# A graph network's edge kernel: the sums of two pairs of edge blocks moved between the first layers of the two pairs

## The chip, the core and the metric

The kernel runs on one core of one Trainium2 chip. A core has five engines with a queue of instructions each: PE (the matrix engine, with its weight loads shown apart as PEld), DVE (vector), ACT (scalar), POOL (here it issues the indirect gathers) and SP (here it issues plain DMAs). An engine works through its queue in order and waits for another one by a semaphore. The metric is the device time of one launch in microseconds (us). A profiled execution gives the time of every instruction; its rows are quoted below.

## The reference

A network of 6,250 nodes with 256 values each and 206,250 edges. What is computed, cut to what matters:

```python
h = relu(layernorm(x))
e = relu(raw @ W_e1.T + b_e1) @ W_e2.T + b_e2          # raw: 64 values of an edge
edge_emb = (e * (polarity + 0.01)) @ W_le.T + b_le
msg = relu(h[src] + edge_emb)                          # one row of h per edge: a gather
aggr = segment_sum(msg, dst, num_segments=6250)        # edges come sorted by dst
x + W_g2 @ relu(layernorm((h + aggr) @ W_g1.T + b_g1)) # per node
```

All numbers are 32-bit floats. The second layer of an edge and `W_le` are one product in the kernel, since nothing nonlinear stands between them.

## The kernel before, in words

The edges are cut into blocks of 512; there are 403 blocks. Two blocks are a pair (`q`, 202 pairs, one DMA for the 64 raw values of both), and half a block (256 edges) is a unit (`u`), so a pair has four units. Almost the whole time goes to one loop over the units in `gnn_kernel`. No planner reorders anything: what the program calls first stands first in each engine's queue.

- **First layer**, `first_layer(q)` (lines 278 to 311): for each half `c` of the 256 outputs one matmul per block (L292, 64 rows by 128 columns of the array, 512 edges wide), so four instructions and four PSUM banks a pair. A 32-bit matmul instruction shows as two records in the profile, so a pair has 8 records and each of them a weight load. ACT reads three of the four banks (L308), DVE the fourth (L305), both into the tile `e`.
- **Second layer of a unit**, `edge_part(u)` (L317 to L334): four matmuls over the full array (L325, 8 records) into one PSUM bank, which DVE adds to `msg` (L331).
- **PSUM**: seven banks `pz` are handed out in a ring (`Ring`); who takes a bank waits until the reader of seven banks ago is done. The eighth bank, `pd`, holds the sums.
- **Message**, `whole(u)`: DVE multiplies by the polarity and adds the gathered rows (L685, tile `hg`), ACT takes the relu (L690).
- **Sums**, `sums` = `add_pairs` (L735 to L753) with `add_up`: per block four matmuls of 128 rows by 32 columns (L703), four of them side by side in the array, 256 wide, into `pd`. Two pairs make 16 instructions, 32 records. The first of a pair waits for the newest message of the pair (`newest`). After every third pair `keep` copies `pd` out on ACT (L718).
- **A turn**, `turn_of(q)`: after the second unit of each pair. In the first and last pairs (`by_two` false) it serves one pair; in the middle, on every second pair, it serves two: 95 such turns, each followed by eight units.
- **Gathers**: `in_step(us, behind)` (L646 to L652), called as `paced` by the first layer and by each unit. It adds the PE work just written down (`spent`: 1.754 us a unit, 0.9 a half of a first layer, 0.46 a block of sums, this one without a call of its own, 0.81 a step of node work) and issues as many gathers (L634, 128 rows of 1 KB each, on POOL) as this work allows at 1.288 us each, with 6 us of float. The first gather of such a call waits until the matmul `behind` is done, the rest follow in POOL's queue.
- **Node work**: transposes and small matmuls (L166, L181, L199, L212) for each group of 128 nodes, spread over the units by `at`, `soon` and `due`.

Of the kernel before, what the change touches and what calls it, by code (L numbers as in the profile page):

```python
# [100 lines left out]
def gnn_kernel(ctx: ExitStack, tc: tile.TileContext, x, src_c, dst_c, dst_r, pol_c, raw_t, w_e1t, w_e2,  # L101
# [37 lines left out]
    def behind(ins, other):  # L139

        if other is not None:
            tc.add_manual_dep(ins.ins, other.ins.name, mybir.DependencyInfo(
                mybir.DependencyClass.Sync, mybir.DependencyReason.DATA), reason="one wait for several")
# [93 lines left out]
    with fast:  # L237
# [35 lines left out]
        def load_pair(q):  # L273
            if q < NP:
                raw[q] = ld.tile([P, 512], F32, name="raw")
                nc.sync.dma_start(out=raw[q], in_=raw_t[q])

        def first_layer(q):

            bs = [b for b in (2 * q, 2 * q + 1) if b < NB]  # L280
            if not bs:
                return
            for b in bs:
                e1[b] = e1_p.tile([P, 2, 512], F32, name="e1")
            pe, z = {}, {}
            for c in range(2):
                olds = []
                for s, b in enumerate(bs):
                    pe[s, c] = ps().rearrange("p a b -> p (a b)")
                    olds.append(ps.old())  # L290
                for s, b in enumerate(bs):
                    z[c] = nc.tensor.matmul(pe[s, c], we1_s[s * F:(s + 1) * F, c * P:(c + 1) * P],  # L292
                                            raw[q][s * F:(s + 1) * F, :], start=True, stop=True)
                    ps.wrote(z[c], len(bs) - 1 - s)
                    reader, writer = olds[s]
                    if reader is not None and writer is not None:
                        tc.declare_no_dep(z[c].ins, writer.ins, reason="the bank's reader has waited for it")
                    if s == 0:
                        for reader, _ in olds[1:]:
                            behind(z[c], reader)  # L300
                paced(LAYER, z[c])
            for c in range(2):
                for s, b in enumerate(bs):
                    if s == c == 1:
                        a = nc.vector.tensor_scalar(e1[b][:, c, :], pe[s, c], be1_s[:, c:c + 1], 0.0, op0=ALU.add,  # L305
                                                    op1=ALU.max)
                    else:
                        a = nc.scalar.activation(e1[b][:, c, :], pe[s, c], AF.Relu, bias=be1_s[:, c:c + 1])  # L308
                    behind(a, z[c])
                    ps.read(a, len(bs) * (1 - c) + len(bs) - 1 - s)  # L310
            raw.pop(q)
# [28 lines left out]
        def by_two(q):  # L340
            return FEW <= q < NP - FEW

        def turn_of(q):


            if not by_two(q):
                if q + 2 < NP:
                    first_layer(q + 2)
                sums(q == NP - 1)
                load_pair(q + 4)  # L350
            elif q % 2 == 0:
                sums(False)
                first_layer(q + 2)
                first_layer(q + 3)
                load_pair(q + 4)
                load_pair(q + 5)

        def forward(u):

            edge_part(u)  # L360
            if u % 4 == TURN:
                turn_of(u // 4)
# [803 lines left out]
```

## Time and profile before

| | |
|---|---|
| median of three runs | 2580.09 us (2572.7 to 2583.99) |
| the profiled execution | 2579.07 us, span 2577.4 us |
| PE busy | 2314.6 us, 90% of the span |
| DVE busy | 1613.4 us, 63% |
| POOL busy | 1618.9 us, 63% |
| ACT busy | 1019.3 us, 40% |
| mean granted clock of PE | 0.946 |

In a row of groups stand the line, the engine, the operation, the tiles written and read, the shape and the count; behind the bar the busy time, the mean of one in ns, and the idle time of the engine just before them with what ended most of it. In a timeline row stand the start and length in us, then engine, line, operation, tiles, shape, the number of records merged into the row, and in brackets the idle time before it and what ended that. A row of waits gives the total in us, the number and the longest. The start of a PE record is when it was taken up; its end is modelled.

### The profile page before, as it was taken

How to read it: one execution, taken by the hardware profiler on the slowest of the kernel's cores; microseconds unless marked ns; L12 is line 12 of the kernel's file. 1: busy time of each engine (PE TensorE's matmuls, PEld its weight loads, DVE VectorE, ACT ScalarE, POOL GpSimd, SP SyncE). 2: the span in 40 equal slices, each digit the busy share in tenths (PEclk: the TensorE clock that was granted, in tenths of full speed). 3: DMA queues.
4: the chain of work that ended last, by engine and by line, in shares of the span. 5: the costliest groups of instructions: out<-in, count | busy, mean ns of one | idle time of the engine just before them, and what ended most of it. 6: DMA issues, size and time to landing. Idle time of an engine off the chain costs nothing.

```text
span 2577.4 us, 36784 instructions
## 1 busy us (share of the span) xinstructions
PE 2314.6 (90%) x11940; PEld 1634.7 (63%) x11940; DVE 1613.4 (63%) x3705; ACT 1019.3 (40%) x1804; POOL 1618.9 (63%) x1675
## 2 busy tenths in 40 slices
PE   9988999989989998988888999998989899888968
PEld 6666666666657666666666666665667566666646
DVE  7866666666656665665656565665656566656636
ACT  7443434343334434343433333343434334333423
POOL 6666666666656666666666666666666666666661
PEclk9899999999989999999999999999999999999989
DMA  9443444434444434443444444444434445443441
GB/s 306 139 135 113 121 123 131 130 115 133 125 118 136 132 112 129 129 132 112 125 125 122 132 134 118 122 130 129 136 115 117 129 123 148 117 132 114 121 119 47
DMA packets 176430, 330.30 MB, mean 128 GB/s; under 512 B 39055, under 2 KB 98280, under 8 KB 176232
## 3 DMA queue, kind: packets, MB, share of 16 engines
q0 software_dynamic: 77376, 211.39, 29.2%
q1 hardware_dynamic: 97556, 113.22, 13.7%
q10 hardware_dynamic: 1300, 3.28, 0.4%
q8 instruction: 95, 1.56, 0.2%
q14 instruction: 103, 0.84, 0.1%
HBM read 293.92 MB, written 33.82 MB: 127 GB/s over the span
## 4 chain that ended last, share of the span: by engine, by line
PE 81%; issue 8%; DVE 5%; another core or an unknown queue 3%; ACT 3%; DMA 0%; ACTq 0%; DVEq 0%
PE pz L325 50%; PE pz L292 17%; PE pd L703 8%; DVE hg L685 2%; PE pz L181 2%; PE pz L212 2%; DVE msg L331 1%; ACT e L308 1%; ACT hg L690 1%; PE pz L166 0%; PE pz L199 0%; DVE st L151 0%; DVE sel L663 0%; ACT xt L440 0%
## 5 line engine op out<-in xcount | busy, mean ns | idle before, releaser
L634 POOL DMA_INDIRECT hg<-hb_d,src_s x1604 | 1574.1, 981 | 897.5 <-issue 520.0
L325 PE MATMUL pz<-wc_s,e 128*128 128x256 f32 x6448 | 1494.5, 388 | 15.5 <-issue 13.0
L325 PEld LDWEIGHTS pz<-wc_s,e 128*128 128x128 f32 x6448 | 1236.4, 194 | 281.6 <-ACT e L308 65.1
L690 ACT ACTIVATE hg<-hg 128x512 f32<-128x512 f32 x805 | 507.5, 630 | 988.5 <-DVE hg L685 800.8
L331 DVE TENSOR_TENSOR msg<-pz,bc_s 128x512 f32<-128x512 f32 x799 | 545.0, 684 | 404.9 <-remote 163.5
L685 DVE SCALAR_TENSOR_TENSOR hg<-msg,pol_s,hg 128x256 f32<-128x256 f32 x1612 | 694.7, 476 | 0.4
L292 PE MATMUL pz<-raw,we_s 64*128 64x512 f32 x1612 | 487.4, 696 | 141.6 <-ACT e L308 86.8
L305 DVE TENSOR_SCALAR e<-pz,vecs 128x512 f32<-128x512 f32 x201 | 150.8, 750 | 504.6 <-PE pz L292 358.4
L308 ACT ACTIVATE e<-pz,vecs 128x512 f32<-128x512 f32 x605 | 367.0, 692 | 202.3 <-PE pz L292 147.9
L292 PEld LDWEIGHTS pz<-raw,we_s 64*128 64x128 f32 x1612 | 177.0, 210 | 395.6 <-issue 232.8
L703 PE MATMUL pd<-hg,sel 128*32 128x256 f32 x3216 | 259.2, 388 | 88.1 <-issue 81.1
L703 PEld LDWEIGHTS pd<-hg,sel 128*32 128x32 f32 x3216 | 110.9, 109 | 216.6 <-issue 163.4
L718 ACT ACTIVATE ms<-pd 128x256 f32<-128x256 f32 x66 | 25.3, 383 | 318.8 <-remote 133.2
L663 DVE SCALAR_TENSOR_TENSOR sel<-iota_w,zero_c,rel 128x128 f32<-128x128 f32 x403 | 137.8, 342 | 0.0
L181 PE MATMUL pz<-wg_s,hT 128*128 128x256 f32 (+1 forms) x196 | 52.8, 393 | 2.6 <-ACT hg L690 2.1
L212 PE MATMUL pz<-wg_s,nT 128*128 128x256 f32 (+1 forms) x196 | 50.8, 382 | 2.0 <-ACT nT L203 1.8
L181 PEld LDWEIGHTS pz<-wg_s,hT 128*128 128x128 f32 (+1 forms) x196 | 37.7, 195 | 10.4 <-ACT hg L690 2.5
L212 PEld LDWEIGHTS pz<-wg_s,nT 128*128 128x128 f32 (+1 forms) x196 | 36.8, 190 | 8.7 <-ACT nT L203 2.7
L444 POOL TENSOR_TENSOR hb<-xt,rows_b 128x256 f32<-128x256 f32 (+1 forms) x49 | 34.1, 728 | 10.5 <-ACT xt L440 4.4
L203 ACT ACTIVATE nT<-pz,vecs 128x128 f32<-128x128 f32 (+1 forms) x98 | 38.7, 444 | 2.6 <-PE pz L199 2.4
L800 DVE TENSOR_TENSOR stb<-stb,ab 128x256 f32<-128x256 f32 x94 | 38.7, 411 | 0.0
L230 DVE SCALAR_TENSOR_TENSOR xt<-xt,zero_c,rows_b 128x128 f32<-128x128 f32 (+1 forms) x98 | 33.5, 343 | 0.0
(108 smaller groups left out, 376.2 us busy)
## 6 DMA issues: line engine op xcount, KB each, us to landing
raw<-in_raw_t_dram SPq DMA_DIRECT2D x202, 256.0 KB
hg<-hb_d,src_s POOLq DMA_INDIRECT x1604
sum_d<-zrow SPq DMA_DIRECT2D x94, 128.0 KB
ab<-sum_d SPq DMA_DIRECT2D x94, 128.0 KB
sum_d<-ms SPq DMA_DIRECT2D x264, 32.0 KB
hb_d<-hb SPq DMA_DIRECT2D x12, 512.0 KB
xt<-in_x_dram SPq DMA_DIRECT2D x48, 128.0 KB
out_dram<-ot SPq DMA_DIRECT2D x48, 128.0 KB
```

The source lines that it names most:

```text
L181: z = nc.tensor.matmul(ph[:n, 0, :], aT[:, c, :n], wg1_s[:, c, :], start=c == 0 and not bias_by_pe, stop=c == 1)
L212: z = nc.tensor.matmul(po[:n, 0, :], nT[:, c, :n], wg2_s[:, c, :], start=c == 0, stop=c == 1)
L292: z[c] = nc.tensor.matmul(pe[s, c], we1_s[s * F:(s + 1) * F, c * P:(c + 1) * P], raw[q][s * F:(s + 1) * F, :], start=True, stop=True)
L305: a = nc.vector.tensor_scalar(e1[b][:, c, :], pe[s, c], be1_s[:, c:c + 1], 0.0, op0=ALU.add, op1=ALU.max)
L308: a = nc.scalar.activation(e1[b][:, c, :], pe[s, c], AF.Relu, bias=be1_s[:, c:c + 1])
L325: last_z = nc.tensor.matmul(pz[:, i, :], e1[b][:, c, k:k + P], wc_s[:, c, :], start=c == 0, stop=c == 1)
L331: ps.read(nc.vector.tensor_add(msg[u], pz, bc_s))
L634: g = nc.gpsimd.indirect_dma_start(out=hg[u][:, i, :], out_offset=None, in_=hb_d, in_offset=bass.IndirectOffsetOnAxis(ap=src_s[:, 2 * u + ...
L663: nc.vector.scalar_tensor_tensor(sel[g][:, k * S:(k + 1) * S, :], iota_w.rearrange("p (o w) -> p o w", o=1).to_broadcast([P, S, W]), zero_ ...
L685: product = nc.vector.scalar_tensor_tensor(hg[u][:, i, :], m[:, i, :], pol_s[:, 2 * u + i:2 * u + i + 1], hg[u][:, i, :], op0=ALU.mult, op ...
L690: done[u] = product, nc.scalar.activation(hg[u], hg[u], AF.Relu)
L703: z = nc.tensor.matmul(acc[g][j * W:(j + 1) * W, :], sel[g][:, k * S + j, :], m[:, j % 2, :], start=k == 0, stop=b == blocks_of(g)[-1])
```

## The change

In a turn for two pairs the call of the sums moves behind the first layer of the first of the two pairs. Nothing else is changed: every instruction is there as before, with the same operands but for the numbers of some buffers.

```diff
             elif q % 2 == 0:
+                first_layer(q + 2)
                 sums(False)
-                first_layer(q + 2)
                 first_layer(q + 3)
                 load_pair(q + 4)
                 load_pair(q + 5)
```

On PE a turn was: 32 records of sums, 16 records of first layer. It becomes: 8 records of first layer, 32 of sums, 8 of first layer. On ACT the copy of `pd` (L718), where a turn has one, moves from ahead of six reads of the first layer to between the third and the fourth. On DVE the order is the same. On POOL the order of the gathers is the same, but the matmuls that they wait for are others: `spent` has the four blocks' 1.84 us of sums added only ahead of the third of the four calls from the first layers, where before it was ahead of the first.

## The prediction

> **What bounds the kernel now.** I read the groups of instructions first (POOL's row from the page, PE's with their shapes apart), then the waits, then the timeline of single turns, PE and POOL apart.
>
> ```profile
> L634 POOL DMA_INDIRECT hg<-hb_d,src_s x1604 | 1574.1, 981 | 897.5 <-issue 520.0
> ...
> L325 PE MATMUL pz<-wc_s,e 128*128 128x256 f32 x6448 | 1494.5, 388 | 15.5 <-issue 13.0 <-ACT msg L329 1.1 <-DVE xt L230 0.9
> L292 PE MATMUL pz<-raw,we_s 64*128 64x512 f32 x1612 | 487.4, 696 | 141.6 <-ACT e L308 86.8 <-issue 44.8 <-DVE msg L331 6.7
> L703 PE MATMUL pd<-hg,sel 128*32 128x256 f32 x3216 | 259.2, 388 | 88.1 <-issue 81.1 <-ACT hg L690 5.2
> ```
>
> PE is the bound, and its second layer (L325) hardly ever waits: 15.5 us of 1494.5. The idle time stands before the first layer (L292) and the sums (L703), both of them in the turns. A turn that nothing disturbs shows what they cost by themselves (PE's rows, then POOL's):
>
> ```profile
> 1044.72 1.93 PE L703 MATMUL pd<-hg,sel 128*32 128x256 f32 x32
> 1046.58 3.70 PE L292 MATMUL pz<-raw,we_s 64*128 64x512 f32 x16
> 1050.22 1.99 PE L325 MATMUL pz<-wc_s,e 128*128 128x256 f32 x8
> ...
> 1042.53 0.95 POOL L634 DMA_INDIRECT hg<-hb_d,src_s  x1 [0.30 <-issue]
> 1045.23 0.95 POOL L634 DMA_INDIRECT hg<-hb_d,src_s  x1 [1.76 <-PE pz L325]
> ```
>
> It takes 1050.22 - 1044.72 = 5.50 us. Over the run L703 and L292 take 259.2 + 88.1 + 487.4 + 141.6 = 976.3 us, busy and idle. At the pace of the free turn they would take 3216/32 x 1.93 + 1612/16 x 3.70 = 567 us. So about 409 us, a sixth of the span, are lost in the turns, some 4.1 us in each; the modelled ends hide part of it as busy time. The usual turn looks like this (PE, ACT, POOL):
>
> ```profile
> 1240.14 1.93 PE L703 MATMUL pd<-hg,sel 128*32 128x256 f32 x32
> 1242.03 2.59 PE L292 MATMUL pz<-raw,we_s 64*128 64x512 f32 x8
> 1244.90 1.15 PE L292 MATMUL pz<-raw,we_s 64*128 64x512 f32 x4 [0.28 <-issue]
> 1247.35 1.13 PE L292 MATMUL pz<-raw,we_s 64*128 64x512 f32 x4 [1.30 <-ACT e L308]
> 1248.41 1.78 PE L325 MATMUL pz<-wc_s,e 128*128 128x256 f32 x7
> ...
> 1246.61 3.58 ACT L308 ACTIVATE e<-pz,vecs 128x512 f32<-128x512 f32 x6 [5.38 <-PE pz L292]
> ...
> 1243.82 0.95 POOL L634 DMA_INDIRECT hg<-hb_d,src_s  x1 [0.30 <-issue]
> 1247.25 0.94 POOL L634 DMA_INDIRECT hg<-hb_d,src_s  x1 [2.49 <-issue]
> ```
>
> The first matmuls of the first layer are through by about 1243, yet ACT, idle for 5.38 us, gets to read them only at 1246.61. What PE has done is told late. The last four records need a bank that ACT has to read first (seven banks, eight are needed), so PE stands from 1246.05 to 1247.35. The telling comes 1246.61 - 1243.82 = 2.79 us after POOL began its last free gather; POOL then stood because its next one hangs on the first layer. In the free turn POOL stood from 1043.48 to 1045.23, just when the sums began, and nothing was late. I read this as: sums issued while POOL gathers without a pause hold back what PE has to tell, until POOL runs out of gathers that it may start. Why that is so the trace does not say. In other turns PE itself gets stuck in the sums (PE, then POOL, then DVE):
>
> ```profile
> 1342.36 1.91 PE L703 MATMUL pd<-hg,sel 128*32 128x256 f32 x26
> 1345.24 0.38 PE L703 MATMUL pd<-hg,sel 128*32 128x256 f32 x1 [0.97 <-issue]
> ...
> 1348.09 0.63 PE L703 MATMUL pd<-hg,sel 128*32 128x256 f32 x3 [0.34 <-issue]
> 1348.65 3.70 PE L292 MATMUL pz<-raw,we_s 64*128 64x512 f32 x16
> 1352.29 1.99 PE L325 MATMUL pz<-wc_s,e 128*128 128x256 f32 x8
> ...
> 1345.22 0.94 POOL L634 DMA_INDIRECT hg<-hb_d,src_s  x1 [0.30 <-issue]
> 1350.08 0.94 POOL L634 DMA_INDIRECT hg<-hb_d,src_s  x1 [3.92 <-ACT ms L718]
> ...
> 1348.12 0.69 DVE L331 TENSOR_TENSOR msg<-pz,bc_s 128x512 f32<-128x512 f32 x1 [6.34 <-remote]
> ```
>
> Again it lets go 2.87 us after the start of POOL's last free gather (1348.09 - 1345.22), and 9.93 us pass from the sums to the second layer. Even the last unit of the second layer, ahead of the sums, DVE gets only then. How often each happens:
>
> ```profile
> PE pz L292 <- ACT e L308: 86.8, 38, 5.0
> ...
> PE pd L703 <- issue: 81.1, 114, 1.9
> ```
>
> 38 waits of the first layer for ACT, at most one a turn, are the first kind; I put the other 57 of the 95 turns down to the second, which overstates it, since some are free or only wait for the newest message.
>
> **The change, part by part.** No instruction is added or removed. F1 to F8 are the eight first-layer matmuls of a turn in their order, two records each.
>
> *One more change of shape on PE.* Before, a turn goes full array, sums, first layer, full array. After it, the first layer stands in two pieces. The end of the kernel has such a piece already:
>
> ```profile
> 2475.38 1.99 PE L292 MATMUL pz<-raw,we_s 64*128 64x512 f32 x8
> 2477.30 1.93 PE L703 MATMUL pd<-hg,sel 128*32 128x256 f32 x32
> 2479.16 2.00 PE L325 MATMUL pz<-wc_s,e 128*128 128x256 f32 x7
> 2482.97 0.38 PE L325 MATMUL pz<-wc_s,e 128*128 128x256 f32 x1 [1.81 <-issue]
> ```
>
> Eight records take 1.92 us from start to start, sixteen in one piece 3.64 (1046.58 to 1050.22). Two pieces cost 2 x 1.92 - 3.64 = 0.20 us more; the sums take 1.86 in both places. Cost: 95 x 0.20 = 19 us, with nothing beside it to hide it.
>
> *The first kind of turn, counted from the end of the second layer (0).* Before: sums at 0, told at 6.47, F7 and F8 at 7.21, second layer at 8.27. Here the bank that F8 needs, and ACT's read of 0.74 us (1246.61 to 1247.35), come after the hold, and so do F7 and F8, 1.06 us. After: F1 to F4 at 0, sums at 1.92, F5 to F8 at 3.78, second layer at 5.70. F8's bank was read by ACT during the sums, so this wait is gone. But POOL has more free gathers: 0.9/1.288 = 0.7 each hang on F1/F2 and on F3/F4, which are now told ahead of the sums, so about two. A gather takes 0.95 us and POOL 0.30 between two, 1.25 us in all, so the last one starts at 3.68 + 2.5 = 6.18 and the hold ends 2.79 later, at 8.97. Who waits then? F8 no longer; the second unit needs the bank of F3, the fourth that of F5. How far PE gets while it is held the last rows show: 7 of the 8 records of the first unit behind the sums, then it stands. So at 8.97 the first unit is all but done, 7/8 x 1.85 = 1.6 us of it (1494.5 us for 6448/8 units). That answers to a second layer begun at 7.4, against 8.27: a gain of 0.9 us. Low end: PE gets only through F8, 8.97 - 8.27, a loss of 0.7. High end: it runs on through the held time, 8.27 - 5.70, a gain of 2.57. I take 0.9, since the late turn has the very order; for 38 turns 34 us, with ends -27 and +98.
>
> *The second kind.* If PE is already held as the turn begins, as at 1342, then F1 to F4 now go through in the held time and their gathers stay shut: let go at 5.73, 0.56 for the rest of the sums (to 1348.65), 1.92 for F5 to F8, second layer at 8.2 and not 9.93, a gain of 1.7. If the hold starts with the sums, it ends 2.5 us later for two more gathers while 1.92 us of first layer stand ahead of it: a loss of 0.6. The trace doesn't settle which; I take the middle, 0.55 x 57 = 31 us, with ends -34 and +97.
>
> *Moved past other queues.* ACT's copy of `pd` waits for the sums and now has three reads ahead of it and three behind; they are of matmuls behind the sums and would wait anyway. F1 to F4 come 1.86 us sooner behind the units whose banks they take; behind DVE's L331 the first layer waited 6.7 us in the whole run, and were that doubled it would not change the sum. SP's loads stand behind both first layers as before. The newest message gets 1.92 us more before the sums ask for it. I cost these at nothing; the cover is the 1.85 us that PE spends on each unit, three of which lie between F4 and the unit whose bank it takes.
>
> Sum: 34 + 31 - 19 = 46 us, so 2579 - 46 = 2533 us. The profiled execution's 2579.07 us is 1 us off the median of 2580.09, so I leave it there. With both low ends it is 2579 + 27 + 34 + 19 = 2659, with both high ends 2579 - 98 - 97 + 19 = 2403.
>
> **Rivals.** *The hold only moves and grows (slower).* It sits at the same sums and ends with POOL's last free gather; F1 to F4 set two more of them free. The price is the two low ends, 2659 us. It decides where PE gets no further than F8 before it stands; for it speaks that the second kind gets stuck within 26 records, against it the late turn with 7 records behind the sums.
>
> *Held time fully covered (much faster).* With F1 to F4 told early, PE has sums, F5 to F8 and three units, 9 us, before it needs anything that is held back. Then 2403. Against it: PE stood after 7 records at 2482.97 with POOL at work.
>
> *Nothing to be won.* POOL needs 16 gathers for eight units, 16 x 1.25 = 20 us of a cycle of 24.4 (1044.72 to 1240.14 are eight cycles), and stands still for the rest until PE tells; if its pauses set the cycle, the gain and the loss cancel: 2579.
>
> *The change of shape is itself the hold.* If the 4.1 us lost in a turn belong to its three changes of shape, 1.4 each, and not to POOL, then a fourth costs 95 x 1.4 = 130 us: 2709. Against it: the free turn has the same three and loses nothing. [...]
>
> **How the numbers follow.** Forecast 2533: 0.40. Much faster, 2403: 0.12. Nothing: 0.13. Hold grows, 2659: 0.27. Shape, 2709: 0.08. About 0.5%, 13 us, is what a measurement here can tell from no change. Faster 0.52, same 0.13, slower 0.35. The range reaches from 2410 to 2660: it leaves out the shape rival and most of the much faster one. The forecast's own range is 2480 to 2570.
>
> **What would show it.** Right: the 86.8 us of L292 behind ACT's L308 go to nearly nothing, eight records of L292 stand at each end of a turn, and what idle time is left stands before L703 and, new, before the first L325 behind a turn. Wrong: L703's idle time and row lengths grow by more than L292's shrink, or L325's idle of 15.5 us grows past 100, or POOL's gathers run through the sums in the turns that were free. If PE's hold has nothing to do with POOL, the 2.8 us from the last free gather to the telling will not be there in the new trace.

## The result and the profile after

The changed kernel takes 2554.2 us (median of four runs, 2549.71 to 2555.42), against 2580.06 us for the kernel before on the same chip: a ratio of 0.990 with a 95% interval of 0.9875 to 0.9925. It is faster, by 26 us or 1%, where 46 us were forecast. The granted clock rose from 0.946 to 0.964.

PE's groups after the change, with their shapes apart, and POOL's gathers from the page:

```profile
L325 PE MATMUL pz<-wc_s,e 128*128 128x256 f32 x6448 | 1506.0, 387 | 60.0 <-issue 46.6 <-ACT e L308 8.6 <-ACT msg L329 1.3
L292 PE MATMUL pz<-raw,we_s 64*128 64x512 f32 x1612 | 462.0, 657 | 66.6 <-DVE msg L331 30.1 <-issue 19.6 <-ACT e L308 5.4
L703 PE MATMUL pd<-hg,sel 128*32 128x256 f32 x3216 | 266.0, 398 | 71.6 <-issue 69.6
L181 PE MATMUL pz<-wg_s,hT 128*128 128x256 f32 x192 | 52.9, 398 | 17.5 <-issue 7.6 <-ACT hT L170 7.1 <-ACT hg L690 2.7
L212 PE MATMUL pz<-wg_s,nT 128*128 128x256 f32 x192 | 50.3, 385 | 5.5 <-ACT nT L203 4.0 <-ACT hg L690 1.4
L199 PE MATMUL pz<-ident,hs 128*128 128x128 f32 x96 | 19.7, 288 | 6.0 <-issue 4.3 <-ACT e L308 1.7
L166 PE MATMUL pz<-ident,stb 128*128 128x128 f32 x94 | 19.0, 277 | 5.0 <-issue 3.6 <-DVE stb L800 1.4
...
L634 POOL DMA_INDIRECT hg<-hb_d,src_s x1604 | 1585.3, 988 | 862.9 <-issue 519.1
```

The same view of the kernel before, for the four groups of node work that the prediction did not show:

```profile
L181 PE MATMUL pz<-wg_s,hT 128*128 128x256 f32 x192 | 51.7, 393 | 2.6 <-ACT hg L690 2.1 <-ACT hT L170 0.5
L212 PE MATMUL pz<-wg_s,nT 128*128 128x256 f32 x192 | 49.7, 381 | 1.0 <-ACT nT L203 0.9 <-issue 0.2
L166 PE MATMUL pz<-ident,stb 128*128 128x128 f32 x94 | 18.9, 283 | 4.1 <-issue 2.9 <-DVE stb L800 1.1
L199 PE MATMUL pz<-ident,hs 128*128 128x128 f32 x96 | 18.9, 279 | 0.0
```

PE takes up its 11940 records in the same order in both traces, but for the sums of 94 turns, which stand where the change puts them. So its busy and idle time by group is an account of the span. In the turns the first layer (L292) falls from 629.0 to 528.6 us, and the sums (L703) from 347.3 to 337.6: 110 us are won. Behind the turns the second layer (L325) grows from 1510.0 to 1566.0, and the node work between its units (L181, L212, L199, L166) from 146.9 to 175.9: 85 us are given back. That leaves 25 us; the two spans differ by 23.7.

One turn of the new order shows both halves (PE, then POOL, ACT and DVE; start and length in us, in brackets the idle time before):

```profile
901.46 1.99 PE L292 MATMUL pz<-raw,we_s 64*128 64x512 f32 x8
903.37 1.93 PE L703 MATMUL pd<-hg,sel 128*32 128x256 f32 x32
905.24 1.99 PE L292 MATMUL pz<-raw,we_s 64*128 64x512 f32 x8
907.15 1.99 PE L325 MATMUL pz<-wc_s,e 128*128 128x256 f32 x8
...
909.20 1.89 PE L325 MATMUL pz<-wc_s,e 128*128 128x256 f32 x8
912.42 5.45 PE L325 MATMUL pz<-wc_s,e 128*128 128x256 f32 x24 [1.32 <-ACT e L308]
920.15 1.60 PE L212 MATMUL pz<-wg_s,nT 128*128 128x256 f32 x4 [2.28 <-ACT nT L203]
...
910.45 0.94 POOL L634 DMA_INDIRECT hg<-hb_d,src_s  x1 [0.30 <-issue]
...
904.96 1.82 ACT L308 ACTIVATE e<-pz,vecs 128x512 f32<-128x512 f32 x3
911.68 1.26 ACT L308 ACTIVATE e<-pz,vecs 128x512 f32<-128x512 f32 x2 [4.90 <-PE pz L325]
...
914.48 0.75 DVE L305 TENSOR_SCALAR e<-pz,vecs 128x512 f32<-128x512 f32 x1 [8.30 <-PE pz L325]
```

ACT reads the first pair's results at 904.96, beside the sums, so the second pair finds its banks free and the turn takes 907.15 - 901.46 = 5.69 us. But what PE has done behind the sums again reaches the others late: the last of the second pair's matmuls is taken up before 907.15, and ACT gets to read them only at 911.68, DVE at 914.48. I call this lateness the hold. After two units the second layer now stands for it, at 912.42, and the node work at 920.15. The hold is still there, two units further on.

### The profile page after: what moved, and what is told of

The parts are those of the page before. It is cut to its first block, busy times and chain, and to the rows that moved or that the text cites. A ratio compares the mean times of both kernels' runs of the same rounds, so it can differ in the third digit from the quotient of the medians.

```text
span 2553.7 us, 36839 instructions
## 1 busy us (share of the span) xinstructions
PE 2312.4 (91%) x11940; PEld 1603.9 (63%) x11940; DVE 1599.9 (63%) x3705; ACT 1012.7 (40%) x1804; POOL 1630.2 (64%) x1675
## 4 chain that ended last, share of the span: by engine, by line
PE 77%; DVE 8%; issue 8%; another core or an unknown queue 3%; ACT 2%; DMA 0%; DVEq 0%; ACTq 0%
PE pz L325 48%; PE pz L292 15%; PE pd L703 8%; DVE hg L685 4%; DVE msg L331 2%; PE pz L181 2%; PE pz L212 2%; ACT hg L690 1%; PE pz L166 1%; ACT e L308 1%; DVE sel L663 1%; PE pz L199 0%; DVE xt L230 0%; DVE stb L800 0%
## 5 line engine op out<-in xcount | busy, mean ns | idle before, releaser
L325 PE MATMUL pz<-wc_s,e 128*128 128x256 f32 x6448 | 1506.0, 387 | 60.0 <-issue 46.6
L325 PEld LDWEIGHTS pz<-wc_s,e 128*128 128x128 f32 x6448 | 1225.5, 193 | 344.1 <-issue 130.9
L690 ACT ACTIVATE hg<-hg 128x512 f32<-128x512 f32 x805 | 507.6, 631 | 980.7 <-DVE hg L685 766.0
L331 DVE TENSOR_TENSOR msg<-pz,bc_s 128x512 f32<-128x512 f32 x799 | 545.4, 685 | 379.0 <-PE pz L325 143.0
L685 DVE SCALAR_TENSOR_TENSOR hg<-msg,pol_s,hg 128x256 f32<-128x256 f32 x1612 | 696.5, 479 | 0.8 <-DMA hg<-hb_d,src_s 0.5
L292 PE MATMUL pz<-raw,we_s 64*128 64x512 f32 x1612 | 462.0, 657 | 66.6 <-DVE msg L331 30.1
L308 ACT ACTIVATE e<-pz,vecs 128x512 f32<-128x512 f32 x605 | 372.7, 684 | 256.6 <-remote 110.1
L703 PE MATMUL pd<-hg,sel 128*32 128x256 f32 x3216 | 266.0, 398 | 71.6 <-issue 69.6
L292 PEld LDWEIGHTS pz<-raw,we_s 64*128 64x128 f32 x1612 | 152.3, 196 | 277.5 <-issue 143.5
L703 PEld LDWEIGHTS pd<-hg,sel 128*32 128x32 f32 x3216 | 118.5, 112 | 244.6 <-issue 201.2
L718 ACT ACTIVATE ms<-pd 128x256 f32<-128x256 f32 x66 | 25.3, 384 | 246.4 <-remote 90.5
L181 PE MATMUL pz<-wg_s,hT 128*128 128x256 f32 (+1 forms) x196 | 54.0, 398 | 17.5 <-issue 7.6
L212 PE MATMUL pz<-wg_s,nT 128*128 128x256 f32 (+1 forms) x196 | 51.5, 385 | 6.4 <-ACT nT L203 4.9
L181 PEld LDWEIGHTS pz<-wg_s,hT 128*128 128x128 f32 (+1 forms) x196 | 35.1, 191 | 33.0 <-ACT hT L170 11.3
L212 PEld LDWEIGHTS pz<-wg_s,nT 128*128 128x128 f32 (+1 forms) x196 | 36.8, 190 | 13.4 <-ACT nT L203 6.4
```

The source lines that it names most:

```text
L181: z = nc.tensor.matmul(ph[:n, 0, :], aT[:, c, :n], wg1_s[:, c, :], start=c == 0 and not bias_by_pe, stop=c == 1)
L212: z = nc.tensor.matmul(po[:n, 0, :], nT[:, c, :n], wg2_s[:, c, :], start=c == 0, stop=c == 1)
L325: last_z = nc.tensor.matmul(pz[:, i, :], e1[b][:, c, k:k + P], wc_s[:, c, :], start=c == 0, stop=c == 1)
L331: ps.read(nc.vector.tensor_add(msg[u], pz, bc_s))
L685: product = nc.vector.scalar_tensor_tensor(hg[u][:, i, :], m[:, i, :], pol_s[:, 2 * u + i:2 * u + i + 1], hg[u][:, i, :], op0=ALU.mult, op ...
L690: done[u] = product, nc.scalar.activation(hg[u], hg[u], AF.Relu)
```

## The experiments

The runs were made in seven sittings, each on one chip. In two of them the kernel before takes 2577 to 2580 us (the sitting of the result above, and that of the run in eight parts below), in the other five 2141 to 2145 us, and within a sitting it hardly varies (2572.7 to 2583.99 us in four runs, 2138.64 to 2146.88 in nineteen). None of the numbers below can be read without this, and it turned out to be the main finding. I compare within a sitting only.

### Without gathers, in both orders

```diff
                 if i == 0:
-                    hg[u] = (hx_p if u % HG < RAW else hg_p).tile([P, 2, D], F32, name="hg")
-                g = nc.gpsimd.indirect_dma_start(...)
+                    if u < HG:
+                        kept[u] = hg_p.tile([P, 2, D], F32, name="hg")
+                        nc.gpsimd.memset(kept[u], 0.0)
+                    hg[u] = kept[u % HG]
```

The order of before:

> The order of before, with the 1604 indirect gathers of the main loop on POOL left out: 16 tiles of gathered rows are kept and used over and over, so the term h[src] of the messages is wrong after the first units. Theory A (POOL's gathers, issued without a pause, hold back what PE has to tell around the sums): with no gathers there is no hold. Every turn then runs at the pace of the free turn, 5.50 us instead of a mean of 9.73, 95 x 4.23 = 402 us less, so about 2180 us; idle time before L703 and L292 falls from 229.7 us to under 30. Theory B (the change of shape between full array, sums and first layer is itself the hold): the turns stay at 9.7 us and the time within 2% of 2580 us. Theory C (the hold belongs to PE's own backlog of untold instructions, whoever runs beside it): also about 2580 us.

The order of after:

> The order of after, with the same gathers left out as in the run beside it. Theory A: again no hold, and of the change only its one more change of shape is left, 95 x 0.20 = 19 us: some 2200 us, slower than the order of before without gathers by 10 to 25 us, so the gain of 26 us turns into a loss. Theory B: no hold goes away, and the order of after stays ahead by about 26 us as with gathers. Theory C: as B. A fourth possibility, that the gain came from reads of banks that ACT now does during the sums and not from the hold, would leave the order of after ahead here too, by up to 38 waits of 1.06 us = 40 us.

They took 2115.62 and 2129.74 us, but before took 2145.13 us in this sitting, so there was no hold that could go away, and the question that these two runs were made for stayed open. What they do show, with one run each, is the price of the new order by itself. The groups of PE (shapes apart), first of the order of before, then of that of after, both without gathers:

```profile
L292 PE MATMUL pz<-raw,we_s 64*128 64x512 f32 x1612 | 378.7, 605 | 6.3 <-DVE msg L331 3.4 <-ACT xt L440 1.4 <-ACT e L308 0.9
L701 PE MATMUL pd<-hg,sel 128*32 128x256 f32 x3216 | 194.5, 382 | 2.2 <-ACT hg L688 2.2
```

```profile
L292 PE MATMUL pz<-raw,we_s 64*128 64x512 f32 x1612 | 402.9, 616 | 4.8 <-ACT e L308 1.9 <-DVE msg L331 1.9 <-DMA raw<-in_raw_t_dram 1.0
L701 PE MATMUL pd<-hg,sel 128*32 128x256 f32 x3216 | 194.5, 382 | 0.2 <-ACT hg L688 0.2
```

The new order is 14 us slower. The first layer's time grows by 24.2 us, part of it by the modelled ends of records, and 3.5 us of waits go. Without a hold and without gathers the change is a loss.

### Plain transfers in the place of gathers

```diff
-                g = nc.gpsimd.indirect_dma_start(...)
+                g = nc.gpsimd.dma_start(out=hg[u][:, i, :], in_=hb_d[(2 * u + i) % 48 * P:((2 * u + i) % 48 + 1) * P, :])
```

> The order of before, each indirect gather of 128 rows replaced by a plain transfer of 128 KB of neighbouring rows, issued from the same queue on POOL at the same places and with the same waits; the indices are left out, so h[src] is wrong. It tells apart POOL's work on a gather (0.95 us of POOL each, 1574.1 us in the run) and the bytes that it moves. If the work on POOL makes the hold, the hold goes: near the run without gathers, 2180 to 2300 us. If the transfers and their landing make it, it stays: within 2% of 2580 us.

2111.86 us, in the same sitting. Again there was no hold to remove. But with the bytes of the gathers still moved, the 33 us to before went all the same: a plain transfer takes POOL 537 ns (856.2 us busy for 1604), a gather 978.

### No gather set free just ahead of the sums

```diff
-            paced(EDGE, last_z)
+            paced(EDGE, last_z, by_two(u // 4) and u % 8 in (0, 1))
...
-                while (got - 2 * RAW) * STEP < spent + AFLOAT and ...:
+                while not shut and (got - 2 * RAW) * STEP < spent + AFLOAT and ...:
```

> The order of before, all gathers kept, but none is set free by the last two units of the second layer ahead of a turn; those gathers hang on the first layer's matmuls behind the sums instead, so POOL stands still while the sums are issued. Theory A: the turns come near the free turn, 5.5 to 7 us instead of 9.73, worth 95 x 2.7 to 4.2 = 260 to 400 us; what the gathers that pile up behind the sums cost in the second layer is open, and takes back at most as much as after's second layer grew, 0.98 us a turn, 93 us. So 2180 to 2410 us. Theories B and C: no change in the turns; the gathers come later, so 2580 us or slower.

2147.69 us against 2145.13. Timed in another sitting:

> The order of before with no gather set free by the last two units ahead of a turn, timed. On a chip where before takes 2580 us, theory A: turns of 5.5 to 7 us, 2180 to 2410 us; if the hold isn't tied to POOL's gathers, 2580 us or slower. On a chip where before takes 2145 us: within 0.5% of it, since there is no hold to take away.

2143.08 us against 2141.46, a ratio of 1.0009 with an interval of 0.9998 to 1.0021: nothing, as expected where before takes near 2141 us. It tells nothing of the hold. Nor did POOL stand still: in the trace of the first of these runs it starts one or two gathers within the 1.93 us of the sums in each of the 94 turns for two pairs that have sums (the first of the 95 has none yet).

### Both kernels in a sitting without the hold

> The changed kernel once more, beside before. The four runs before this one were on a chip on which before took 2145.13 us and not 2580.06, at a granted clock of 0.995 and not 0.946. If the hold exists on this call's chip (before near 2580): the ratio is 0.99 again. If it doesn't (before near 2145): theory A gives only the one more change of shape, 95 x 0.15 = 14 us as between the two runs without gathers, 2159 us, ratio 1.006 to 1.009. Rival: the moved reads of banks gain by themselves, then the ratio is under 1 here too.

> The kernel before, for its trace on this call's chip. If before takes near 2145 us: all 95 turns at 5.5 to 6 us, idle before L703 and L292 under 30 us together instead of 229.7, and PE's completions told as they come although POOL gathers through the sums; that would say that POOL's gathers without a pause aren't enough for the hold. If near 2580: as the trace shown.

After takes 2139.73 us and before 2141.46: a ratio of 0.9983, interval 0.9973 to 0.9994. The loss of 14 us that was expected did not come; it is a gain of 2. The ratio is under 1, as the rival had it, but POOL's row below gives another reason than the moved reads. Of the second expectation, the idle time holds (23.9 us, under 30) and the turns hold in the main: 78 of the 94 with sums take 6 us or less, and the longest 10.6. Groups of before in this sitting (POOL's from the page, PE's with shapes apart):

```profile
L634 POOL DMA_INDIRECT hg<-hb_d,src_s x1604 | 1567.9, 978 | 494.1 <-issue 349.5
...
L325 PE MATMUL pz<-wc_s,e 128*128 128x256 f32 x6448 | 1455.2, 382 | 0.0
L292 PE MATMUL pz<-raw,we_s 64*128 64x512 f32 x1612 | 386.3, 613 | 16.3 <-ACT e L308 8.4 <-DVE msg L331 6.5 <-DMA raw<-in_raw_t_dram 1.5
L703 PE MATMUL pd<-hg,sel 128*32 128x256 f32 x3216 | 195.9, 383 | 7.6 <-ACT hg L690 7.6
```

The same of after:

```profile
L634 POOL DMA_INDIRECT hg<-hb_d,src_s x1604 | 1565.9, 976 | 493.7 <-issue 339.7
...
L292 PE MATMUL pz<-raw,we_s 64*128 64x512 f32 x1612 | 406.5, 619 | 12.1 <-ACT e L308 4.7 <-DVE msg L331 4.6 <-DMA raw<-in_raw_t_dram 2.7
L703 PE MATMUL pd<-hg,sel 128*32 128x256 f32 x3216 | 194.5, 382 | 0.6 <-ACT hg L690 0.6
```

The same program, with the same gathers, now has 606.1 us of first layer and sums where it had 976.3. A turn of before, PE, POOL and ACT:

```profile
1959.74 1.93 PE L703 MATMUL pd<-hg,sel 128*32 128x256 f32 x32
1961.61 3.71 PE L292 MATMUL pz<-raw,we_s 64*128 64x512 f32 x16
1965.24 1.99 PE L325 MATMUL pz<-wc_s,e 128*128 128x256 f32 x8
...
1959.76 1.08 POOL L634 DMA_INDIRECT hg<-hb_d,src_s  x1 [0.30 <-issue]
1961.15 1.02 POOL L634 DMA_INDIRECT hg<-hb_d,src_s  x1 [0.30 <-issue]
...
1962.85 3.58 ACT L308 ACTIVATE e<-pz,vecs 128x512 f32<-128x512 f32 x6 [0.37 <-PE pz L292]
```

POOL gathers straight through the sums, and yet the turn takes 5.50 us and ACT reads the first results 1.24 us after the first layer began. So gathers beside the sums are not enough for a hold.

POOL's row says what seems to set the time here. A pause of 0.30 us stands before each gather, 481 us for 1604, and POOL's idle time is hardly more: 494.1 us. Busy and idle, POOL's gathers fill 2062.0 us of the span of 2140.4 before, and 2059.6 of 2140.8 after. PE is close behind: the order of before has a span of 2113.6 us without gathers and of 2109.9 with plain transfers, some 30 us less. I take it that what the new order does to PE, for the worse by its shapes and for the better by 11 us of waits (23.9 to 12.7), comes out of this slack.

### The sums behind both first layers

```diff
                 first_layer(q + 2)
-                sums(False)
                 first_layer(q + 3)
+                sums(False)
```

> The sums moved one place further: the first layers of both pairs, then the sums, then the second layer. The first layer stands in one piece again, so a turn has the three changes of shape of before and not the four of after, and the sums ask for the newest message 3.64 us later than before. On a chip where before takes near 2141 us: theory A (a change of shape costs 14 to 19 us in the run, the later request for the message gives back some 17): 14 to 19 us less than after, 2121 to 2126 us, ratio 0.990 to 0.993; if a new wait comes in (the eighth matmul of the first layer needs a bank, and the sums in turn stand ahead of the second layer), no gain. On a chip where before takes near 2580 us: the hold comes with the sums, and nothing of the first layer is left to be done while it lasts, so the loss in the turns moves wholly into the second layer: 2554 to 2600 us.

> The same order with the gathers of the main loop left out (16 tiles of gathered rows used over and over, so h[src] is wrong after the first units). On a chip where before takes near 2580 us: theory A, no hold without gathers, 2110 to 2150 us; if the hold isn't POOL's, 2500 us and more. On a chip where before takes near 2141 us: as the order of before without gathers, 0.986 of before, and not 0.993 as the order of after without them, if the number of changes of shape is all that is between these.

With gathers it takes 2154.26 us against 2143.58, a ratio of 1.0046, interval 1.0031 to 1.0061: slower. The 14 to 19 us less than after that theory A gave did not come; the new wait that the expectation allowed for did. Without them 2116.7 us, 0.9875 of before, close to the 0.9862 of the order of before without gathers and not the 0.9928 of the order of after. So the first layer in one piece does give back what its second piece cost; what the order loses, it loses only with the gathers in place:

```profile
L634 POOL DMA_INDIRECT hg<-hb_d,src_s x1604 | 1570.9, 979 | 501.1 <-issue 342.0
...
L292 PE MATMUL pz<-raw,we_s 64*128 64x512 f32 x1612 | 392.6, 618 | 33.2 <-DVE msg L331 22.8 <-ACT e L308 6.2 <-DMA raw<-in_raw_t_dram 2.7
```

POOL's stream has become 2072.0 us long, 10 us longer than before's 2062.0, and the kernel is 10.7 us slower. The tiles of gathered rows come free with the sums, and these now come later. The wait of the first layer behind DVE's message (22.8 us against 6.5) is the other new thing; which of the two leads I did not separate.

### Eight parts in one run, with the hold

To have every question answered wherever the hold might turn up, one kernel runs eight schemes, 12 turns each:

```diff
+        def part(u):
+            q = u // 4
+            return "gnpqGNPQ"[(q - FEW) * 8 // (NP - 2 * FEW)] if by_two(q) else "g"
...
+                if part(4 * q).isupper():
+                    first_layer(q + 2)
+                    sums(False)
+                else:
+                    sums(False)
+                    first_layer(q + 2)
...
+                if part(u) in "nN":
+                    return
+                if part(u) in "pP":
+                    g = nc.gpsimd.dma_start(...)
```

> One run in eight parts of 12 turns each. Parts 1 to 4 have the order of before, 5 to 8 that of after; within each four: all gathers (1, 5), gathers left out (2, 6), each gather replaced by a plain transfer of 128 KB (3, 7), all gathers but none set free ahead of the sums (4, 8). In parts 2, 3, 6 and 7 h[src] is wrong. On a chip where before takes near 2580 us: theory A says turns of 9.7 us in part 1, 5.5 in part 2, 5.5 to 7 in part 4, 8.4 in part 5, 5.7 in part 6; part 3 tells whether the work of the gather on POOL or the transfer matters. If the hold isn't POOL's: 9.7 in parts 1 to 4. On a chip where before takes near 2141 us: there POOL gathers without any pause from 200 us to the end (1604 x (0.978 + 0.30) = 2050 us), so theory F is that POOL sets the time and not PE: a cycle of a turn and eight units then takes 16 x 1.28 = 20.5 us on average in parts 1 and 5 alike, whatever the order, and PE's own pace in parts 2, 3 (order of before) and 6, 7 (order of after, 0.15 to 0.20 us a turn longer).

This sitting had the hold: before took 2576.98 us, the run in parts 2360.43. Stretches of the profile from turn to turn, one for each part (bounds and length in us, then the busy time of PE, PEld, DVE, ACT and POOL, the granted clock of PE, the share and rate of the DMA engines):

```profile
99.83:404.72 304.89, 273.69 (x1414) 190.62 (x1413) 198.95 (x444) 116.79 (x202) 196.29 (x199) 0.93 0.45 129
428.11:656.59 228.48, 228.48 (x1322) 170.95 (x1321) 175.24 (x402) 109.38 (x193) 0.59 (x1) 1.00 0.16 49
656.59:904.57 247.98, 247.98 (x1434) 185.44 (x1433) 187.47 (x427) 119.88 (x211) 103.55 (x192) 1.00 0.50 151
904.57:1209.51 304.94, 275.63 (x1417) 189.81 (x1416) 183.92 (x418) 115.94 (x205) 190.66 (x196) 0.96 0.43 125
1209.51:1500.84 291.33, 270.81 (x1428) 188.07 (x1427) 188.25 (x430) 118.23 (x208) 178.99 (x180) 0.99 0.42 123
1500.84:1750.37 249.53, 249.53 (x1418) 183.88 (x1417) 186.26 (x424) 119.62 (x208) 12.91 (x24) 1.00 0.20 62
1750.37:2004.58 254.21, 252.79 (x1439) 185.21 (x1438) 183.85 (x420) 118.81 (x208) 115.25 (x194) 1.00 0.49 146
2004.58:2229.55 224.97, 201.09 (x1057) 139.14 (x1056) 138.94 (x316) 87.91 (x154) 142.69 (x147) 0.98 0.43 125
```

The first turn of part 2, in which gathers of part 1 are still under way, is left out. The stretches hold 12, 11, 12, 12, 12, 12, 12 and 9 turns, so a cycle takes 25.41, 20.77, 20.67, 25.41, 24.28, 20.79, 21.18 and 25.00 us. In the order of before PE stands for 31.2 us of part 1 and for nothing at all in parts 2 and 3; in that of after, 20.5 us in part 5, nothing in part 6 and 1.4 in part 7. The granted clock goes with it: 0.93 in part 1, 1.00 without gathers. The turns alone, which the expectation gave, take 10.1 us on average in part 1, 8.7 in part 4, 8.1 in part 5 and 5.7 in part 6; part 4 is the miss.

So without gathers there is no hold, and with plain transfers of the same size, from the same queue at the same places (151 GB/s, more than the 129 of part 1), there is none either. It isn't the bytes, then, and not POOL issuing transfers as such; it goes with the indirect gathers, which all the slow parts have and none of the fast ones. (The last turn of part 7 already has gathers for part 8.) One thing stays mixed in: a plain transfer takes POOL less time, so POOL is busy for 103.55 us of 247.98 in part 3 and for 196.29 of 304.89 in part 1. Whether the kind of transfer counts or the time that POOL is busy with it, this run does not tell. A turn of part 2 and one of part 6:

```profile
492.92 1.93 PE L720 MATMUL pd<-hg,sel 128*32 128x256 f32 x32
494.79 3.70 PE L292 MATMUL pz<-raw,we_s 64*128 64x512 f32 x16
498.42 0.92 PE L325 MATMUL pz<-wc_s,e 128*128 128x256 f32 x3
...
1585.10 1.99 PE L292 MATMUL pz<-raw,we_s 64*128 64x512 f32 x8
...
1590.80 1.56 PE L325 MATMUL pz<-wc_s,e 128*128 128x256 f32 x6
```

5.50 and 5.70 us, the two paces by which the prediction reckoned. So the turn's added change of shape costs 0.20 us in this trace too; what takes that time no row shows.

Part 4 was to have POOL still at the sums, and the cycle is that of part 1. But POOL wasn't still (PE, then POOL):

```profile
1004.07 1.07 PE L720 MATMUL pd<-hg,sel 128*32 128x256 f32 x16
1008.03 1.07 PE L720 MATMUL pd<-hg,sel 128*32 128x256 f32 x16 [2.88 <-issue]
...
1005.00 0.95 POOL L651 DMA_INDIRECT hg<-hb_d,src_s  x1 [0.30 <-ACT rs L156]
1006.26 1.01 POOL L651 DMA_INDIRECT hg<-hb_d,src_s  x1 [0.30 <-issue]
1007.58 0.95 POOL L651 DMA_INDIRECT hg<-hb_d,src_s  x1 [0.30 <-issue]
```

It still had gathers in its queue from earlier units. This part leaves open whether a POOL that is silent during the sums would take the hold away.

### Fewer gathers, smaller sums, other orders

```diff
+            return "gdecAFGg"[(q - FEW) * 8 // (NP - 2 * FEW)] if by_two(q) else "g"
...
+                if part(u) in "de" and got % 4 == 0:
+                    return
...
+                    if part(2 * b) == "c" and j > 0 and k > 0 and b != blocks_of(g)[-1]:
+                        continue
```

> Again one run in eight parts of 12 turns each. Order of before: 1 all as before; 2 every fourth gather left out; 3 every fourth gather left out and none set free by the last two units ahead of a turn, so that POOL, which then has time to spare, should stand still at the sums; 4 all gathers, but half of the sums' matmuls left out (in four blocks of six only one of four); 5 the sums behind both first layers; 6 the sums of one pair, the second pair's first layer, the sums of the other pair; 7 the order of after; 8 as part 1. The results of parts 2 to 4 are wrong for what is left out. On a chip where before takes near 2577 us: theory A (gathers issued while the sums are) gives turns of 10 us in parts 1 and 8, 8 to 10 in part 2, 5.5 to 6.5 in part 3 and 8.4 in part 7. If the gathers' share of the time counts and not where they stand, parts 2 and 3 agree. Part 4: if the burst of small matmuls is needed beside the gathers, 5 to 7 us; if not, near 9.5. Parts 5 and 6 tell which order loses least: a cycle of under 24.3 us (that of after) would be better than both. On a chip where before takes near 2141 us: cycles of 20.5 us in parts 1, 4, 5, 6, 7 and 8, which POOL sets, and 20.3 in parts 2 and 3, where it has time to spare.

> The kernel of the run before again, for another chip: 1 order of before; 2 every fourth gather left out; 3 the same, and none set free by the last two units ahead of a turn; 4 half of the sums' matmuls left out; 5 the sums behind both first layers; 6 the sums of the two pairs apart; 7 the order of after; 8 as part 1. Where before takes near 2577 us: theory A gives turns of 10 us in parts 1 and 8, 8 to 10 in part 2, 5.5 to 6.5 in part 3, where POOL stood from 2.5 us ahead of the sums to 3.3 us behind their start in 9 of 12 turns of the run before; if not where the gathers stand counts but how many there are, parts 2 and 3 agree. Part 4 near 5 us if the burst of small matmuls is needed, near 9.5 if not. Parts 5 and 6 against the 24.3 us a cycle of the order of after. Where before takes near 2141 us: cycles of 20.6 to 21.0 us in all parts, as in the run before.

Both times the sitting had no hold: 2134.95 us against 2140.71, and 2134.28 against 2142.45. The parts came out alike, with cycles of 20.6 to 21.0 us in the first run and 20.6 to 21.1 in the second, close to what was expected for that case; parts 2 and 3, where POOL has time to spare, take 20.9 and 20.7 us and not the 20.3 expected. The question on the hold (gathers beside the sums, or gathers at any place; the burst of small matmuls or any matmul) stays open. The second of these ran on a chip of the same number as the run with the hold, some 13 minutes later. If the same number means the same chip, which the record does not say, the hold doesn't simply belong to a chip.

## Why the prediction was right, and where not

- **The bound and the loss.** The 409 us lost in the turns were read rightly, as time by which PE is late and not time that the work needs: in the sittings without the hold first layer and sums take 606.1 us instead of 976.3, not far from the 567 reckoned.
- **"Sums issued while POOL gathers without a pause hold back what PE has to tell."** Half of it is shown. The gathers are needed (parts 2, 3, 6 and 7). They aren't enough: the turn at 1959.74 has them and no hold. That the sums matter has only been argued, from the place where the hold begins. The trace of before fits it: of the 94 turns with sums, the 8 in which no gather starts within the first 1.93 us of the sums take 7.1 us on average, the other 86 take 10.0. Whether PE's work is told late or done late the rows can't say either, since the end of a PE record is modelled. Not everything is late: where ACT waits for DVE's L685, it starts L690 at most 0.38 us behind its end, in the trace of before as in the one without the hold. What else has to come together, and what differs between sittings, the runs don't show.
- **One more change of shape, 19 us.** Right: 5.70 against 5.50 us a turn, 95 x 0.20 = 19 us. Without gathers the whole kernel lost 14.
- **The first kind of turn, 34 us.** The mechanism was right. ACT reads the first pair's banks beside the sums, and the wait of L292 for ACT's L308 falls from 86.8 to 5.4 us. The rows of the turn at 901.46 are those that were foreseen, with eight records of L292 at each end.
- **The second kind, 31 us.** The weakest step. The sums, where these turns were to lose less, take 337.6 us instead of 347.3, and their idle time "issue" 69.6 instead of 81.1. Counted in the traces, turns whose sums take over 2.5 us from the first record to the last are 49 of those 94 before (57 were reckoned) and 38 after. Such a turn lasts 10.3 us before and 10.6 after, so the 0.55 us that each was to gain did not come; all other turns fall from 9.2 to 7.1.
- **The signs named.** Idle time is new before L325, 60.0 us and not past 100. The 2.8 us from POOL's last free gather to the telling are no fixed time. In the turn at 901.46 ACT and PE follow the gather at 910.45 by 1.2 and 2.0 us. Over all turns in which ACT, having stood for over 2 us, first reads more than 2.5 us behind the start of the first layer, it reads 0.7 to 4.2 us behind the start of a gather before the change (20 turns) and 0.4 to 3.3 after it (17 turns), 2.6 in the median both times. One sign of being wrong did show: in the turn at 901.46 POOL starts a gather every 1.25 us or so from 901.58 to 910.45, right through the sums, and the turn itself takes 5.69 us.
- **Together.** The two kinds were to bring 65 us. In the account of the span, turns with the change of shape taken out gain 110 + 19 = 129 us, and 85 are lost behind them, so 44 remain. What was mis-sized is what the held time costs the second layer: "7 of the 8 records of the first unit behind the sums, then it stands" rested on a single turn. In the turn at 901.46 PE does two units, then stands several times, for ACT's reads and for the node work too, which my sum did not have at all: 29 of the 85 us. That 26 us came out near 46 is thus in part luck: more was won in the turns than reckoned, and more lost behind them.
- **Other queues, nothing.** Too low. L292 behind DVE's L331 went from 6.7 to 30.1 us, where a doubling was allowed for. The cover of 1.85 us a unit doesn't cover a hold that is several units long, since then the reader of the bank is itself late.
- **The rivals.** That the hold only moves was half right: it moved behind the turn, without growing. That the change of shape is itself the hold is refuted, by turns of 5.50 and 5.70 us with the same changes. That POOL's pauses set the cycle and nothing is to be won is wrong with the hold. Without it POOL's gathers and their pauses do seem to set the time, and the gain is 0.2%.
- **What the prediction couldn't see.** Every number in it came from a sitting with the hold. The gain of 1% is the gain there.

No order tried here beats both kernels: the one with the sums last loses 0.5% where it was timed, and none but the order of after was measured against before where the hold is.

## What to carry to other kernels

When an engine stands for reasons that its own program doesn't explain, run the unchanged kernel again at another time and on another chip before reordering work around it: here the same program took 2580 or 2141 us, and the difference of 17% was some seventeen times what the reordering won. The reordering that hid a wait in this kernel moved it to the next consumers: the idle time before L292 fell from 141.6 to 66.6 us, that before L325 rose from 15.5 to 60.0 and that before the node work from 7.7 to 34.0. So follow what is late next through as many units as the wait is long, node work included. And an account of one in-order engine, group by group with busy and idle time added, shows in a few rows what was won and where it was given back.

## What the runs showed of the hardware that was not expected

- The same kernel takes 2577 to 2580 us in some sittings and 2141 to 2145 in others, with granted clocks, for this kernel, of 0.946 to 0.948 and 0.994 to 0.998. The lower clock goes with PE standing: in one and the same run it is 0.93 with gathers and 1.00 without.
- In the sitting of the eight parts, PE stands for 31.2 us in the 12 turns with 128-row indirect gathers on POOL and not at all with plain transfers of 128 KB in their place. In the sittings without the hold the same gathers, at 978 ns each for 981, go with 23.9 us of idle time before first layer and sums in the whole run, against 229.7 with it.
- The trace of before has 1230 records of PE's counter of finished work in the sitting with the hold, 292 of them less than 100 ns behind the one before; without the hold it has 1502, and 11 so close. ACT's and DVE's counters lose records too (1073 for 1750 instructions that raise it, and 2037 for 3523), but only 0 and 9 of theirs stand so close together, and DVE's work reaches ACT on time (L690 starts at most 0.38 us behind the end of L685). So of these three only PE's reports come in bunches, and the missing records by themselves are no sign of a late engine. Every execution here was recorded, so no run shows whether the recording itself has a part in the hold.
- A gather takes POOL 0.98 us and 0.30 us of pause stands before each. 1604 of them fill 2060 us of a span of 2140, and by the rows that is what bounds this kernel where nothing holds PE back, with PE's own pace some 30 us under it.
